# Splitting a third block product of the experts' first layer, with its sums on GpSimd

## The chip, the cores and the metric

The kernel runs on one core of a Trainium2 chip. Its time is device time in microseconds (us). The core has a matrix engine (TensorE, in the profile PE, its weight loads PEld), a vector engine (VectorE, DVE), a scalar engine (ScalarE, ACT), a general engine (GpSimd, POOL) and a queue engine (SyncE, SP). Matrix products go into PSUM banks, from which DVE and ACT read.

## The reference

The reference is one layer in float32 for 4096 tokens of width 512. A normalised `x` attends to 3202 rows of context, a gated sum is added to `x`, and a mixture of experts follows:

```python
xf = _layernorm(x).reshape(4096, 512)
gates = softmax(xf @ w_router + b_router)          # 8 experts
topv, topi = top_k(gates, 2)
cap = 640                                          # int(1.25 * 4096 / 8)
buf = each token's row into its expert's slots, up to cap
h = gelu(buf[e] @ w1[e] + b1[e])                   # 640 x 512 @ 512 x 2048
out = h @ w2[e] + b2[e]                            # 640 x 2048 @ 2048 x 512
y = the two outputs of each token, weighted by its gates and normalised
x = x + tanh(g_ffn) * y
```

The change touches the routing in one place, and otherwise the first of the two products of each expert, `buf[e] @ w1[e]`, and its gelu.

## The kernel before

The kernel has three stages in time. The attention takes the first 1480 us or so. The routing follows, to about 1577. Then come the experts, one after the other, each some 120 us, to about 2549.

**The routing.** The 32 tiles of 128 tokens are done in steps of 4, 4, 4, 4, 3, 3, 3, 3, 2 and 2 tiles (`STEPS`). For each tile `tile_mm` multiplies with the router and output weights (the PE rows `x1p`, L1755). For the step before, DVE picks the best two experts (`choose`, L1822 to L1843), and PE counts how many tokens each expert has so far with two small matmuls (`place`, L1870 and L1871, the second is `prev.counted`). POOL sends the rows to the experts' slots (L1904). The call `tc.issue_after` pins an instruction behind another on its engine; the order of PE's work in this stage is written with it. `idle_work(mm, n)` (L88) issues `n` matmuls 128x512 on constants behind `mm`; before the change it is used only where the first expert comes in.

**The experts' first layer.** It is computed transposed: `w1` is the weight operand, and the 640 slots, 320 at a time, are the moving operand. 2 x 2 blocks of `w1` and of the slots are multiplied with 7 block products in place of 8 (Strassen's scheme in Winograd's form), which needs sums of blocks of `w1` (`w1_sums`, L1652 to L1655) and of the slots (`x_forms`) beforehand, and sums of the products behind. A block product here is two program matmuls of 128x320, and the trace has two rows for each f32 matmul, so 4 rows. `hidden(e, idx)` does one step: all seven products for one 128-row block of each half of the output. There are eight steps, idx 0 to 7. In one step PE does the products in the order 0, 3, 4, 1, 5, 6, 2. They go to banks X, Q, Y, X, Z, Y and W. Three of the banks receive a copy before they are added to: ACT copies X into Y after product 0 (L2301), Y into Z after product 4 (L2310), and Z into W or into `hi` after product 5 (L2327). ACT also copies Q into `p5` (L2305), which DVE adds to the results (L2318, L2328, L2332), and does the gelus (L2315, L2325, L2329, L2335, L2336). Gelus that wait for a DVE sum are kept in a list `owed`; `due(n)` issues the first `n` of them.

**The products split deeper.** In steps 0 to 5 (`idx < DEEP_IDX`) the products 6 and 2 are not done step by step. A pair of steps (pair 0 to 3) is treated as a 2 x 2 problem again: seven program matmuls of 128x160 instead of eight of 128x320, in three stages `first`, `second` and `third` from `parts`, interleaved with the other products of steps 1 to 6 by `step(i)`. They need further sums: `deep_w` (L2210 to L2213, four of 128x128 for each pair and product) and `deep_x` (L2197 to L2200, four of 128x160 for each expert and product), all on DVE. Their results are copied by ACT (L2234, L2238) and added by DVE (L2246 to L2249). Steps 6 and 7 do the products 6 and 2 undivided for themselves, and no part of a split product is interleaved with step 7.

**The order.** Within the experts the order on PE, ACT and DVE and of the loads is written out by hand: `pe`, `ac`, `dv` and `ld` each append to a chain (`chained`), every instruction pinned behind the one before. POOL gathers the rows to be added to (`accs`, L2435) and scatters them at the expert's end (L2508).

**The first expert.** Its slots arrive while the routing ends. `first_expert_in` transposes them, does some early products, then DVE makes `x_forms` and the 20 small operations of `coefs(0)` (gate coefficients and row numbers, L2091 to L2094), and after those the deep sums of the first pair. The gathers of L2435 need the row numbers.

Of the kernel before, what the change touches and what calls it, by code (L numbers as in the profile page):

```python
# [9 lines left out]
ALU = mybir.AluOpType  # L10
# [4 lines left out]
P = 128  # L15
# [5 lines left out]
def gated_layer(ctx, tc, x, x_t, ctxt, ctxt_t, ctxt_c, ctxt_r, g_xattn, g_ffn, w_sim, w_sim_r, b_sim, W_qv, W_qv_t, b_qv, b_qv_c, w_router, b_router, w1, b1, w2, b2, out):  # L21
# [1638 lines left out]
    with ExitStack() as s2:  # L1660
# [279 lines left out]
        for g in range(len(STEPS)):  # L1940
            s.next = begin(g + 1) if g + 1 < len(STEPS) else None
            if prev is not None:
                choose(prev)
            ahead = min(3, s.n)
            for i in range(ahead):
                mm = tile_mm(s, i)
            if s.n > 2:
                with tc.issue_after(mm.ins):
                    place_prev()
                if s.n == G and routed:  # L1950
                    with tc.issue_after(scaled[-1].ins):
                        send(2)
                for i in range(ahead, s.n):
                    tile_mm(s, i)
            with tc.issue_after(scatters[-1]) if s.n == G and scatters else ExitStack():
                sc = scale(s)
            scaled.append(sc)
            if s.n == 2:
                with tc.issue_after(mm.ins):
                    place_prev()  # L1960
                mm = prev.counted
            if s.next is None:

                s.first = ps_mm.tile([P, 2, 512], F32, name="first", tag="mm")[:, 0, :E]
                with tc.issue_after(mm.ins):
                    mm = nc.tensor.matmul(s.first, ones, s.base[:, 0, :], start=True, stop=True)
            elif g + 2 == len(STEPS):

                cnt = ps_mm.tile([P, 2, 512], F32, name="cnt", tag="mm")[:, 0, :E]
                with tc.issue_after(mm.ins):  # L1970
                    mm = nc.tensor.matmul(cnt, ones, s.base[:, 0, :], start=True, stop=True)
                s.lift = small("lift", [P, s.n, E])
                stt(s.lift[:, 0, :], cnt, 1.0 / P, second, ALU.mult, ALU.max)
            with tc.issue_after(sc.ins):
                send(len(routed) if s.next is None else 4 if s.n == 2 else 7)
            prev, s = s, s.next
# [19 lines left out]
    with ExitStack() as s3:  # L1996
# [133 lines left out]
        def first_expert_in():  # L2130

            behind = None
            for s in range(NST):
                load = rows_in(0, s) if s else first_rows[0]
                row_loads.append(load.ins)

                near = (s + 1) * P <= CAP - len(late) // 2 * P
                if near:
                    tc.declare_no_dep(
                        load.ins, group="late" if s else "middle", reason="the last steps' rows lie behind these"  # L2140
                    )
                for i in scatters + (middle if s or not near else []) + ([] if near else late):
                    tc.add_manual_dep(
                        load.ins, i.name, mybir.DependencyInfo(mybir.DependencyClass.Sync, mybir.DependencyReason.DATA),
                        reason="every token is in its slot",
                    )
                if behind is None:

                    behind = prev.counted
                with tc.issue_after(behind.ins):  # L2150
                    ps = transposed(ps_tr, xb_of[0, s], f"bps0_{s}")
                dst = bT[:, :, s * P : (s + 1) * P]
                if s == NST // 2:
                    nc.scalar.copy(dst[:, :2, :], ps[:, :2, :])
                    with tc.issue_after(nc.vector.tensor_copy(dst[:, 2:, :], ps[:, 2:, :]).ins):
                        w_ops.pop(0)()
                else:
                    (nc.vector.tensor_copy if s % 2 else nc.scalar.copy)(dst, ps)
                behind = moved[-1] if s else idle_work(moved[-1], 2)
                for cols, q, f in WORK.get(s, ()):  # L2160
                    B = [bT[:, k, :HC] for k in ((2, 3) if q else (0, 1))]
                    behind = early_product(q, f, B, cols, behind, cols.start > 0)
            tail["pe"] = behind
            for op in x_forms():
                tail["dv"] = op()
            dv(*coefs(0))

        first_expert_in()
        with tc.issue_after(row_loads[-1]):
# [4 lines left out]
        def rows_of(ti, s):  # L2174
# [9 lines left out]
            k: (b, [flat_set[i][:, q * HH : (q + 1) * HH] for q in range(3)] + [p7[:, i - 5, :HH]])  # L2184
            for k, i, b in (("2", 5, xT[2]), ("6", 6, B22))
        }

        def w_of(k, pair):
            n = 3 * (2 * (pair % 2) + (k == "6"))
            return [flat_set[2 + (n + q) // 4][:, (n + q) % 4 * P : ((n + q) % 4 + 1) * P] for q in range(3)]  # L2190

        def deep_x(k):

            b, (t1, t2, t4, t3) = x_of[k]
            b11, b12, b21, b22 = (b[:, c, d : d + HH] for c in range(2) for d in (0, HH))
            return [
                lambda: tt(t1, b12, b11, ALU.subtract),  # L2197
                lambda: tt(t2, b22, t1, ALU.subtract),
                lambda: tt(t3, b22, b12, ALU.subtract),
                lambda: tt(t4, b21, t2, ALU.subtract),  # L2200
            ]

        def deep_w(e, k, pair):

            a = w1_forms(e, pair // 2)[int(k)]
            f = pair % 2 * 2 * P
            a11, a12, a21, a22 = (a[:, c, f + r : f + r + P] for r in (0, P) for c in range(2))
            s1, s2, s4 = w_of(k, pair)
            return [
                lambda: tt(s1, a21, a22, ALU.add),  # L2210
                lambda: tt(s2, s1, a11, ALU.subtract),
                lambda: tt(a21, a11, a21, ALU.subtract),
                lambda: tt(s4, a12, s2, ALU.subtract),  # L2213
            ]

        def parts(e, k, pair, c_bank):

            XWQ = ps_tr.tile([P, DC, P], F32, name=f"d{e}_{k}{pair}", tag="tr").rearrange("p c t -> p (c t)")
            X, W, Q = (XWQ[:, i * HH : (i + 1) * HH] for i in range(3))
            YZ = banks[c_bank][:, : 2 * HH]  # L2220
            Y, Z = YZ[:, :HH], YZ[:, HH:]
            a = w1_forms(e, pair // 2)[int(k)]
# [2 lines left out]
            s1, s2, s4 = w_of(k, pair)  # L2225
            b, (t1, t2, t4, t3) = x_of[k]
            b11, _, b21, b22 = (b[:, c, d : d + HH] for c in range(2) for d in (0, HH))
            dst = hT[:, 0, 2 * pair : 2 * pair + 2, HC:] if k == "6" else hT[:, 1, 2 * pair : 2 * pair + 2, :HC]

            def first():  # L2230
                mm(X, a11, b11, True, True)
# [9 lines left out]
            def third():  # L2241
                mm(Z, s3, t3, False, True)
                mm(Y, s4, b22, False, True)

            adds = [
                lambda: tt(dst[:, :, HH:], dst[:, :, HH:], Q.unsqueeze(1).to_broadcast([P, 2, HH]), ALU.add),  # L2246
                lambda: tt(dst[:, :, :HH], dst[:, :, :HH], XWQ[:, : 2 * HH].rearrange("p (f t) -> p f t", f=2), ALU.add),
                lambda: tt(dst[:, 0, HH:], dst[:, 0, HH:], Y, ALU.add),
# [2 lines left out]
                    Z.unsqueeze(1).to_broadcast([P, 2, HH]), ALU.add,  # L2251
                ),
            ]
            return first, second, third, adds, dst

        def hidden(e, idx):

# [11 lines left out]
            if 1 <= idx <= DEEP_IDX:  # L2269
                k, pair = ("6", idx // 2) if idx % 2 else ("2", idx // 2 - 1)  # L2270
                part = parts(e, k, pair, 5 if split else 2 + (idx + 1) % 2)

            def product(ps, k, start=False):
                for i in range(2):
                    mm(ps, A[k][i], XS[{2: 6, 6: 2}.get(k, k)][i], start and i == 0, i == 1)

            def step(i):
                if part:
                    part[i]()

# [15 lines left out]
            else:  # L2296
# [4 lines left out]
                    ac(lambda: nc.scalar.copy(Y, X))  # L2301
                step(0)
                due(1)
                product(Q, 3, True)
                ac(lambda: nc.scalar.copy(p5, Q))  # L2305
                step(1)
                if not part:
                    due(1)
                product(Y, 4)
                ac(lambda: nc.scalar.copy(Z, Y))  # L2310
                step(2)
                due(1)
            if not there:
                product(X, 1)
                ac(lambda: nc.scalar.activation(lo[:, :HC], X, AF.Gelu, bias=b_lo))  # L2315
            due(len(owed))
            if split:
                dv(lambda: tt(lo[:, HC:], Y, p5, ALU.add))  # L2318
# [108 lines left out]
        for e in range(E):  # L2427
# [2 lines left out]
                ld(lambda: load_w2(e, 0), lambda: load_w2(e, 1))  # L2430
            b2_t = sb.tile([P, D], F32, name=f"b2_{e}", tag="b2", bufs=1)
            ld(lambda: nc.sync.dma_start(b2_t, b2[e].partition_broadcast(P)))
            cf, ti = cf_of[e], ti_of[e]
            for s in range(NST):
                gather = nc.gpsimd.indirect_dma_start(  # L2435
# [12 lines left out]

            (B11w, B12w, B21w, B22w), right, inner = output(e)
            bias = [add(s, slice(None), b2_t) for s in range(NST)]  # L2450
            dv(*deep_w(e, "6", 0), *deep_x("6"))
            if e:
                dv(*w1_sums(e, 0, 2))
            for idx in range(2 * KQ):
                if more and idx == 2:
                    ld(*[lambda s=s: rows_in(e + 1, s) for s in range(NST - 1)])
# [6 lines left out]
                    dv(*deep_w(e, "2", 0), *deep_x("2"))  # L2463
                if idx in (1, 3):
                    dv(*deep_w(e, "6", 1 + idx // 2), *deep_w(e, "2", 1 + idx // 2))
                if idx in (4, 6, 7):
                    k = (0, 2, 4)[(4, 6, 7).index(idx)]
                    dv(left(1, k, k + 2), left(3, k, k + 2))
# [175 lines left out]
```

## Time and profile before

| | |
|---|---|
| median of three runs | 2552.36 us (2552.12 to 2552.47) |
| profiled execution | 2551.32 us, span 2549.5 us |
| busy time of TensorE, VectorE, ScalarE, GpSimd | 2531.7, 1974.8, 715.8, 275.5 us |
| mean granted TensorE clock | 0.999 |

The profile is of one execution. In the views by instruction a row gives the start from the span's beginning, the time from start to end, the engine, the line in the kernel, the operation, the tile written and the tile read, the shape, and how many neighbouring instructions of the same kind are merged into it (x8). A bracket behind it tells how long the engine was idle before and which engine's instruction ended that. Matmul rows overlap one another, so the distance between starts is what one costs, not the row's own duration. In the table by stretches the columns are the busy time of PE, PEld, DVE, ACT and POOL with the number of instructions, the granted clock of TensorE as a share of full speed, the share of the DMA engines, and the GB/s moved.

### The profile page before, as it was taken

The page shows a single profiled execution, that of the slowest core. Times are in us where ns is not written, and L with a number is a line of the kernel's source. Part 1 is how long each engine was busy: PE and PEld are TensorE (multiplying, and loading weights), DVE is VectorE, ACT ScalarE, POOL GpSimd, SP SyncE. Part 2 cuts the span into 40 slices and gives each one's busy share as a digit, 9 for nine tenths or more (in the row PEclk, how much of TensorE's full clock was granted, in tenths as well). Part 3 has the DMA queues.
Part 4 walks back from the last instruction along what each step waited for, and adds up shares of the span by engine and source line. Part 5 has one row for each costly group of instructions (what it writes and reads, how often), then busy time and mean ns, then how long its engine had stood idle before and what let it go on. Part 6 is the DMA issues. An engine that isn't in the chain of part 4 may idle for free.

```text
span 2549.5 us, 37831 instructions
## 1 busy us (share of the span) xinstructions
PE 2531.7 (99%) x14256; PEld 2214.7 (87%) x14256; DVE 1974.8 (77%) x4118; ACT 715.8 (28%) x1556; POOL 275.5 (11%) x399
## 2 busy tenths in 40 slices
PE   9999999999999999999999999999999999999998
PEld 7788888998988988989989887798888888888978
DVE  8887865876967868859658657887888888787877
ACT  1112302323123123123231144424232332424150
POOL 0101220001001000000000056010101010101010
PEclk9999999999999999999999999999999999999999
DMA  7568795875976957758748895322313141414120
GB/s 265 194 215 295 268 350 175 281 266 167 317 226 205 307 194 241 265 188 285 249 154 292 272 353 190 130 100 95 133 67 133 71 156 43 162 42 158 47 103 21
DMA packets 198407, 489.08 MB, mean 192 GB/s; under 512 B 22462, under 2 KB 79102, under 8 KB 196176
## 3 DMA queue, kind: packets, MB, share of 16 engines
q1 hardware_dynamic: 151984, 386.37, 45.0%
q0 software_dynamic: 21696, 59.07, 6.4%
q10 hardware_dynamic: 24544, 41.21, 4.4%
q8 instruction: 113, 1.85, 0.3%
q14 instruction: 70, 0.57, 0.1%
HBM read 397.40 MB, written 97.52 MB: 194 GB/s over the span
## 4 chain that ended last, share of the span: by engine, by line
PE 89%; issue 5%; DVE 4%; POOL 1%; DMA 1%; ACT 0%; POOLq 0%; SPq 0%; DVEq 0%
PE bank L2027 30%; PE bank L761 21%; PE bank L984 13%; PE bank L1153 6%; PE bank L1510 5%; PE x1p L1755 2%; PE bank L1254 2%; PE d L2027 2%; PE p7d L1510 1%; PE p4d L1510 1%; PE bank L813 1%; PE v L1254 1%; PE bps L2103 1%; DVE SM L1023 1%; PE bank L990 1%
## 5 line engine op out<-in xcount | busy, mean ns | idle before, releaser
L761 PE MATMUL bank<-Qp,kt 128*128 128x256 f32 x1344 | 305.2, 379 | 0.0
L761 PEld LDWEIGHTS bank<-Qp,kt 128*128 128x128 f32 x1344 | 254.4, 190 | 34.1
L2027 PE MATMUL bank<-w,hT 128*128 128x256 f32 (+1 forms) x1280 | 260.7, 359 | 0.7 <-ACT u L2519 0.7
L2027 PEld LDWEIGHTS bank<-w,hT 128*128 128x128 f32 x1280 | 223.8, 190 | 27.4 <-ACT u L2519 1.1
L761 PE MATMUL bank<-q,kt 128*128 128x256 f32 x1008 | 231.3, 379 | 0.0
L761 PEld LDWEIGHTS bank<-q,kt 128*128 128x128 f32 x1008 | 191.5, 190 | 26.0
L2027 PE MATMUL bank<-bT,w 128*128 128x320 f32 x736 | 211.1, 432 | 0.6 <-ACT bank L2310 0.6
L984 PE MATMUL bank<-dt,vf 128*128 128x128 f32 x1680 | 204.8, 275 | 0.0
L984 PEld LDWEIGHTS bank<-dt,vf 128*128 128x128 f32 x1680 | 196.0, 192 | 0.0
L2027 PEld LDWEIGHTS bank<-bT,w 128*128 128x128 f32 x736 | 136.6, 190 | 50.5 <-ACT bank L2310 1.1
L2027 PE MATMUL bank<-XT,w1s 128*128 128x320 f32 x512 | 156.4, 433 | 0.1
L804 DVE TENSOR_TENSOR M<-M,E_all 128x1024 f32<-128x1024 f32 x80 | 97.9, 1223 | 46.0 <-ACT E_all L721 44.6
L2508 POOL DMA_INDIRECT out<-acc,ti x40 | 39.7, 992 | 806.7 <-DVE acc L2447 800.0
L1755 PE MATMUL x1p<-W,q2T 128*128 128x264 f32 x512 | 117.7, 391 | 3.0 <-DVE lg L1777 1.8
L717 DVE TENSOR_TENSOR E_all<-bank,p5s 128x512 f32<-128x512 f32 x42 | 28.9, 688 | 113.4 <-ACT bank L716 113.3
L1755 PEld LDWEIGHTS x1p<-W,q2T 128*128 128x128 f32 x512 | 97.7, 192 | 20.1 <-PE pos L1871 1.8
L2027 PEld LDWEIGHTS bank<-XT,w1s 128*128 128x128 f32 x512 | 91.9, 190 | 25.9 <-ACT bank L2286 0.5
L891 DVE TENSOR_TENSOR E_all<-E_all,mb 128x1024 f32<-128x1024 f32 x84 | 101.2, 1211 | 10.3 <-ACT mb L866 10.3
L984 PE MATMUL bank<-E_all,vf 128*128 128x128 f32 x828 | 106.5, 275 | 0.0
L892 ACT ACTIVATE E_all<-E_all 128x1024 f32<-128x1024 f32 x84 | 88.8, 1057 | 49.8 <-DVE E_all L891 49.3
L984 PEld LDWEIGHTS bank<-E_all,vf 128*128 128x128 f32 x828 | 99.8, 192 | 0.3
L2027 PEld LDWEIGHTS bank<-l,l 128*128 128x128 f32 x736 | 92.9, 192 | 7.6
(644 smaller groups left out, 4955.1 us busy)
## 6 DMA issues: line engine op xcount, KB each, us to landing
vf<-vf_d SPq DMA_DIRECT2D x122, 768.0 KB
kt<-kt_d SPq DMA_DIRECT2D x84, 512.0 KB
w<-in_w SPq DMA_DIRECT2D x16, 2048.0 KB
w<-in_w SPq DMA_DIRECT2D x32, 1024.0 KB
kt<-in_ctxt_t SPq DMA_DIRECT2D x84, 384.0 KB
wp<-wt_d SPq DMA_DIRECT2D x56, 520.0 KB
buf_d<-zero SPq DMA_DIRECT2D x80, 129.0 KB
xb<-buf_d SPq DMA_DIRECT2D x39, 258.0 KB
```

The source lines that it names most:

```text
L717: tt(dst(1, 1), Z, p5, ALU.add)
L761: nc.tensor.matmul(ps[:, jl, :], kts[j][:, KSLOT[p], k, :], B[p][:, k, :], start=start and jl == 0 and k == 0, stop=stop and k == 1, skip_ ...
L804: tt(M, M, e[:, :, h], ALU.max)
L891: live[g]["last"] = tt(e, e, m, ALU.subtract)
L892: live[g]["exp"] = nc.scalar.activation(e, e, AF.Exp)
L984: nc.tensor.matmul(ps, a[:, j, :], rhs[r][:, j, :], start=start and j == 0, stop=j == NP - 1 and (rest is None or add is None), skip_group ...
L1153: nc.tensor.matmul(ps[b], vt[:, j - i * JH, b * P : (b + 1) * P], right(j) if j < NJ else right_c, start=start and j == 0 and b == 0, stop ...
L1254: mm = nc.tensor.matmul(acc[k][:, b, :], a[:, b * P : (b + 1) * P], r, start=start and b == 0, stop=stop, skip_group_check=True,)
L1510: nc.tensor.matmul(ps[m], A[p][:, k, m * P : (m + 1) * P], wt[:, k, :], start=start and k == 0, stop=stop and k == DC - 1, skip_group_chec ...
L1755: mm = nc.tensor.matmul(ps[:, j, :B1], qTs[g][:, c, q * P : (q + 1) * P], W1[:, c, j, :], start=(c == 0), stop=(c == DC - 1))
L2027: return chained("pe", lambda: nc.tensor.matmul(ps, a, b, start=start, stop=stop, skip_group_check=True))
L2508: sc = nc.gpsimd.indirect_dma_start(out=out[:, :], out_offset=rows_of(ti, s), in_=accs[s][:, :], in_offset=None, bounds_check=N - 1, oob_i ...
```

## The change

It has three parts.

The first is in the experts' first layer. Product 3 is split deeper in the same way as products 6 and 2, for pairs 1, 2 and 3 of every expert but the first, and for pairs 2 and 3 of the first: 23 pairs. Its three stages (`extra`) are all done in the even step of the pair, interleaved with the rest, and product 3 into Q is left out in both steps. Its results go into both `p5` buffers by three more ACT copies and two more DVE adds (in place of the two copies of Q). Its sums are made by GpSimd in a chain of its own (`gp`): four of 128x160 at each expert's start and four of 128x128 for each pair, ahead of and behind the gathers and between them. In the steps concerned only one owed gelu is issued ahead of `lo`'s gelu, and all others behind it.

The second is the first expert's order on DVE: the deep sums of its first pair now come before `coefs(0)`, not behind.

The third is in the routing: where a step of 3 tiles follows one of 4, one `idle_work` matmul is issued behind the count `prev.counted`.

```diff
@@ routing
                 with tc.issue_after(mm.ins):
                     place_prev()
+                if prev is not None and prev.n > s.n:
+                    mm = idle_work(prev.counted, 1)
@@ first_expert_in
             for op in x_forms():
                 tail["dv"] = op()
-            dv(*coefs(0))
@@ deep sums
+        flat_low = [t.rearrange("p a b -> p (a b)") for t in sets[0]]
+        x_of["3"] = (xT[0], [flat_low[6][:, q * HH : (q + 1) * HH] for q in range(3)] + [u2[:, 0, :HH]])
+
+        def third_split(e, idx):
+            return idx >= (KQ if e == 0 else 2)
...
-        def deep_x(k):
+        def deep_x(k, tt=tt):
...
-        def deep_w(e, k, pair):
+        def deep_w(e, k, pair, tt=tt):
@@ parts
-            X, W, Q = (XWQ[:, i * HH : (i + 1) * HH] for i in range(3))
+            X, W, Q = (XWQ[:, i * HH : (i + 1) * HH] for i in ((2, 0, 1) if k == "3" else (0, 1, 2)))
...
+            def copies():
+                nc.scalar.copy(p5s[1], XWQ[:, : 2 * HH])
+                nc.scalar.copy(p5s[0][:, :HH], X)
+                return nc.scalar.copy(p5s[0][:, HH:], Q)
+
             adds = [
+                lambda: tt(p5s[0][:, HH:], p5s[0][:, HH:], Y, ALU.add),
+                lambda: tt(
+                    p5s[1].rearrange("p (d t) -> p d t", d=2), p5s[1].rearrange("p (d t) -> p d t", d=2),
+                    Z.unsqueeze(1).to_broadcast([P, 2, HH]), ALU.add,
+                ),
+            ] if k == "3" else [
@@ hidden
+            triple = third_split(e, idx)
+            extra = parts(e, "3", idx // 2, 1) if triple and idx % 2 == 0 else None
...
             def step(i):
+                if extra:
+                    extra[i]()
                 if part:
                     part[i]()
...
                 step(0)
                 due(1)
-                product(Q, 3, True)
-                ac(lambda: nc.scalar.copy(p5, Q))
-                step(1)
-                if not part:
-                    due(1)
+                if not triple:
+                    product(Q, 3, True)
+                    ac(lambda: nc.scalar.copy(p5, Q))
+                    step(1)
+                    if not part:
+                        due(1)
                 product(Y, 4)
                 ac(lambda: nc.scalar.copy(Z, Y))
-                step(2)
-                due(1)
+                step(1 if triple else 2)
+                if not triple:
+                    due(1)
             if not there:
                 product(X, 1)
                 ac(lambda: nc.scalar.activation(lo[:, :HC], X, AF.Gelu, bias=b_lo))
+            if triple:
+                step(2)
+            if extra:
+                ac(extra[5])
+                dv(*extra[3])
             due(len(owed))
@@ the loop over experts
+            if e:
+                dv(*deep_w(e, "6", 0), *deep_x("6"), *w1_sums(e, 0, 2))
+
+            def third_w(pair):
+                return chained("gp", *deep_w(e, "3", pair, nc.gpsimd.tensor_tensor))
+
+            chained("gp", *deep_x("3", nc.gpsimd.tensor_tensor))
+            if third_split(e, 2):
+                third_w(1)
+            if e == 0:
+                dv(*deep_w(0, "6", 0), *deep_x("6"), *coefs(0))
             cf, ti = cf_of[e], ti_of[e]
             for s in range(NST):
                 gather = nc.gpsimd.indirect_dma_start(
...
-            dv(*deep_w(e, "6", 0), *deep_x("6"))
-            if e:
-                dv(*w1_sums(e, 0, 2))
...
                     dv(*deep_w(e, "6", 1 + idx // 2), *deep_w(e, "2", 1 + idx // 2))
+                if idx in (3, 5):
+                    third_w(1 + idx // 2)
```

More of the change, by code (lines that the diff above doesn't have):

```diff
@@ L2186, in gated_layer @@
         }
+        flat_low = [t.rearrange("p a b -> p (a b)") for t in sets[0]]
+        x_of["3"] = (xT[0], [flat_low[6][:, q * HH : (q + 1) * HH] for q in range(3)] + [u2[:, 0, :HH]])
+        def third_split(e, idx):
+            return idx >= (KQ if e == 0 else 2)
         def w_of(k, pair):
+            if k == "3":
+                return [flat_low[4 + pair % 2][:, q * P : (q + 1) * P] for q in range(3)]
             n = 3 * (2 * (pair % 2) + (k == "6"))
             return [flat_set[2 + (n + q) // 4][:, (n + q) % 4 * P : ((n + q) % 4 + 1) * P] for q in range(3)]
-        def deep_x(k):
+        def deep_x(k, tt=tt):
             b, (t1, t2, t4, t3) = x_of[k]
@@ L2227, in parts @@
             b11, _, b21, b22 = (b[:, c, d : d + HH] for c in range(2) for d in (0, HH))
-            dst = hT[:, 0, 2 * pair : 2 * pair + 2, HC:] if k == "6" else hT[:, 1, 2 * pair : 2 * pair + 2, :HC]
+            dst = None if k == "3" else hT[:, 0, 2 * pair : 2 * pair + 2, HC:] if k == "6" else hT[:, 1, 2 * pair : 2 * pair + 2, :HC]
             def first():
@@ L2253, in parts @@
             ]
-            return first, second, third, adds, dst
+            return first, second, third, adds, dst, copies
         def hidden(e, idx):
```

## The prediction

> **What bounds the kernel now.** I read the page first, for the engines' shares and the clock, then the table by stretches of the span, then the instructions in order of time at the three places that the change touches. The page and the table, the table's columns being the busy time of PE, PEld, DVE, ACT and POOL, the granted clock, and DMA:
>
> ```profile
> PE 2531.7 (99%) x14256; PEld 2214.7 (87%) x14256; DVE 1974.8 (77%) x4118; ACT 715.8 (28%) x1556; POOL 275.5 (11%) x399
> ...
> 2000.00:2500.00 500.00, 499.32 (x2843) 426.04 (x2842) 412.84 (x911) 161.20 (x410) 40.68 (x40) 1.00 0.26 95
> ```
>
> TensorE is the bound, and in the experts it has no gaps: 499.32 us of 500, with VectorE busy for 412.84 and GpSimd for 40.68. So matmul time taken out there is worth its full length, as long as no new wait opens. In the same way every new wait of PE costs its full length; nothing lies behind PE to absorb it. So I look for each bank that a matmul must wait for after the change. Step 7 of the second expert's first layer (`hidden(e, 7)`, the last unsplit step), in order of time:
>
> ```profile
> 1757.04 2.32 PE L2027 MATMUL bank<-XT,w1s 128*128 128x320 f32 x8
> 1757.24 0.41 ACT L2301 COPY bank<-bank 128x320 f32<-128x320 f32 x1 [2.82 <-PE bank L2027]
> ...
> 1759.19 2.32 PE L2027 MATMUL bank<-bT,w 128*128 128x320 f32 x8
> 1759.39 0.41 ACT L2310 COPY bank<-bank 128x320 f32<-128x320 f32 x1
> ...
> 1760.47 0.53 ACT L2315 ACTIVATE hT<-bank,b_t 128x320 f32<-128x320 f32 x1 [0.19 <-PE bank L2027]
> 1760.90 0.55 ACT L2335 ACTIVATE hT<-hT,b_t 128x320 f32<-128x320 f32 x1
> ...
> 1761.35 0.52 ACT L2336 ACTIVATE hT<-bank,b_t 128x320 f32<-128x320 f32 x1
> 1761.90 0.41 ACT L2327 COPY bank<-bank 128x320 f32<-128x320 f32 x1
> ...
> 1762.42 1.01 PE L2027 MATMUL bank<-XT,w 128*128 128x320 f32 x3
> ```
>
> The reader should see two things. The eight rows from 1757.04 are product 3 (into Q) and product 4 (onto Y). Product 4 needs Y, which ACT copies out of X until 1757.65; product 3 hides that. And the last copy, of Z into W, ends at 1762.31, only 0.12 before its matmuls start at 1762.42: ACT is just in time here, although two of its five owed gelus (L2325) ran earlier in the step.
>
> **Durations of PE.** One f32 matmul of the program is two rows. Eight rows of width 320 take 2.15 us (1757.04 to 1759.19), .2692 a row; the start distance at width 160 is .1358. After a wait the first rows take .104 longer (.373 against .269).
>
> **Part 1, the third product.** A pair of steps has product 3 twice: 8 x .2692 = 2.153 us. Split deeper it is 7 program matmuls of width 160: 14 x .1358 = 1.901. That is .252 us less per pair; 2 pairs in the first expert and 3 in each of the other seven make 23, so -5.80 us. With each goes work for the others. ACT has five copies in place of two: per pair about 1.5 us against .85, in idle time (161.20 of 500). DVE has two more adds, .32 + .49, hidden in its 87 idle us of 500 but moving other adds back by .8 per pair. GpSimd has 16 sums per expert (12 in the first) that are not in the trace in this form.
>
> The wait that it adds, first place: step 7 has no part of a deep product to put between, since parts are issued in steps 0 to 6. Without product 3 it goes from product 0 straight to product 4, which waits for the copy of Y. PE would be free where product 3 starts now, 1757.040; the copy ends at 1757.650, and PE restarts .053 after such a copy elsewhere (1592.907 to 1592.960), so at 1757.703. That is .663 + .104 = .767 us, in each of 8 experts. In steps 3 and 5 the other part's first stage (six rows of 160, .81) covers the .663 with .15 over; steps 2, 4 and 6 have two stages there.
>
> Second place, same step: only one owed gelu is issued after product 0; the other four now stand behind `lo`'s gelu. Let T0 be the start of product 5 (1760.27 now). `lo`'s gelu starts at T0 + .20, the four at T0 + .63, 1.07, 1.52 and 1.97 (distances .426, then .445 to .452), the last ends at T0 + 2.49, and the copy of Z into W runs from T0 + 2.52 to 2.93. Product 2 starts at T0 + 2.98 instead of T0 + 2.153 (8 rows): .83 + .104 = .93 us, again 8 times. Queued behind that copy on ACT is the gelu of `hi`, needed only in the second layer's later products; nothing else waits. Bounds for the two together: at least the two bare gaps, 8 x 1.49 = 11.9; at most, with ACT 5% slower, 8 x 1.85 = 14.8. I take 8 x 1.70 = +13.6.
>
> **GpSimd's sums.** The nearest rows are a MEMSET of 128x260, 317 ns, and of 128x512, 559 ns, which read nothing, and a TENSOR_TENSOR of 128x4 with a `pow`, about 1050 ns. Below, at memset speed, a 128x160 sum is about .2 us; above, 1.05. The sums read two operands, as L2197 on DVE does in .32, so I take .45, between these. The first that PE needs (`s2` of pair 1) is needed at 1721.2 in the second expert; behind the gathers at 1.3 us each it is there by 1718.6 to 1719.5. At 1.05 each, the six up to it add 6 x .6 = 3.6 and it comes 1.0 to 1.9 us late. I cost it at nothing: the cover is the 1.7 to 2.6 us left, and if that goes PE waits in step 2, seven times, up to +13 us; below nothing there is no reason for. The scatters and gathers on the same queue move back by four to six sums, 1.8 to 2.7 us; the gathers start at 1715.4 in the second expert and their rows are first used at 1756.8 (L2447), so that is hidden.
> The trace shows no wide GpSimd sum beside a DVE sum. The Trainium skill, "SBUF — State Buffer", section "Who interferes with whom", says that a DVE instruction with two SBUF inputs contends with a GpSimd instruction reading SBUF, one blocking for the whole of the other. This speaks against the change: an estimate from it is that GpSimd's 16 sums could each hold DVE for their length, some 7 us of its 20 idle us per expert, so the sum would still stand unless a late add meets PE.
>
> **Part 2, the first expert.** The chain of waits there, and PE's rows:
>
> ```profile
> 1594.04 0.22 DVE L2094 SCALAR_TENSOR_TENSOR cf<-dc,cf,SX 128x1 f32<-128x1 f32 x1
> ...
> 1594.66 0.43 ACT L2286 COPY bank<-l 128x320 f32<-128x320 f32 x1
> ...
> 1595.52 0.54 PE L2027 MATMUL d<-l,l 128*128 128x160 f32 x2 [0.95 <-issue]
> ...
> 1596.35 0.54 PE L2027 MATMUL d<-l,w1s 128*128 128x160 f32 x2 [0.29 <-DVE p L2199]
> ...
> 1596.73 1.24 PE L2027 MATMUL bank<-XT,w1s 128*128 128x320 f32 x4
> ```
>
> The 20 small coefficient operations hold DVE from 1591.89 to 1594.25; the deep sums, on which the two PE waits rest (1.11 and .46 by starts), end at 1596.30. Moved ahead they are done 2.32 earlier, at 1593.98, before PE can ask (1594.41). Late next is ACT: its copy of the early product ends at 1595.10, so product 3 or 4 starts at about 1595.15 rather than 1596.73 (-1.58). Of this a later copy, queued behind a gelu whose add DVE doesn't do sooner, gives back about .35, and GpSimd's four sums, now beside the deep sums, some .3. I take -.9, between 0 (the sums held by GpSimd as long as by the coefficients) and -1.6. The first expert's five gathers on POOL wait for the coefficients, 2.3 us longer; their rows are used in step 5, some 40 us on.
>
> **Part 3, the matmul on constants in routing.** Two stretches, one window of the clock long each:
>
> ```profile
> 1506.25:1509.66 3.41, 1.48 (x7) 0.81 (x6) 3.03 (x17) 2.23 (x6) 2.56 (x3) 1.00 1.04 427
> 1509.66:1513.08 3.42, 3.21 (x7) 2.53 (x8) 3.04 (x15) 2.20 (x6) 2.49 (x4) 0.50 1.01 390
> ```
>
> After a stretch with PE busy for 1.48 the clock was granted at 0.50 for 3.41 us; the next lowest stretches on the same grid, 2.24, 2.31 and 2.44, were followed by 1.00. In the slow stretch the router's rows stand .44 apart instead of .222: 6 x .218 + .351 = 1.66 us lost. The new matmul (128x512, 2 x .429) runs after the count (L1871) at 1508.88 and is over before 1509.87, where PE next has work, so it costs nothing, and lifts 1.48 to 2.34, among the unthrottled. I take -1.66; bounds 0 (still throttled) and -1.7, and +.1 if it should end late.
> The Trainium skill, "TensorE: Matmul & The Clock Gate", in its part on the two states, calls the 3413 ns window free-running; this trace agrees with the length (3.41). By it the grid falls elsewhere in each run, so a run that is not throttled would have nothing to gain; by the rule alone the term may be anything between 0 and the full loss.
>
> **Sum.** -5.80 + 13.58 - .9 - 1.66 = +5.2 us. The profiled execution took 2551.32 (span 2549.5), the median of the runs is 2552.36, 1.04 more. So about 2556.5 for a profiled execution and 2557.6 for the median. A measurement of this kernel tells about 0.2% (5.1 us, 2547.3 to 2557.5) from no change, and the forecast lies on that edge.
>
> **Rivals.**
> 1. One of step 7's waits is covered: gelus that overlap more closely, say. The row for it is the copy into W that is just in time now; against it stands that four ACT instructions of .445 can't fit in 2.15 with `lo`'s gelu and a copy. The sum falls by 6.1 to 7.4: 2550.2 to 2551.5. Within.
> 2. Both are covered, or the scheduler keeps something between: -5.80 - .9 - 1.66 = 2544.0, faster. It decides only if step 7's product 4 doesn't wait for the copy of Y; against it, ACT stood idle for 2.82 us and began the copy .20 after product 0, so nothing on ACT could bring it earlier.
> 3. GpSimd's sums are late, because they take over .75 to .88 us (.45 and a sixth of the cover), or are held that long by DVE: 1 to 1.9 us of waiting in step 2 of seven experts, 2564.6 to 2570.9, slower.
> 4. Step 7 as forecast, but the clock still drops and the first expert gains little: 2559.5 to 2560.2.
>
> **Chances.** The forecast .48 (its own range 2555.5 to 2559.3, half above the edge), rival 1 .16, rival 2 .10, rival 3 .14, rival 4 .12. The range leaves out most of rival 2 and the upper end of rival 3: 2549 to 2567. Slower: .24 + .14 + .12 = .50; within: .24 + .14 = .38; faster: .12 with the lower end of rival 1.
>
> **What would show it.** In step 7 of each expert, PE rows of product 4 with .6 to .8 us idle behind ACT's copy of Y, and of product 2 with .8 to .9 behind the copy of Z; 14 rows of 160 in place of 8 of 320 in 23 places; no throttled stretch near 1510; the first expert's PE without waits for DVE. Wrong it is if PE waits for POOL (rival 3), or if step 7 has no such gaps.

## The result and the profile after

The changed kernel takes 2560.75 us (median of 7 runs, 2560.16 to 2563.55), the kernel before 2552.33 on the same chip. The ratio is 1.0038, 95% interval 1.0028 to 1.0048 (the ratios given here are worked out from all the runs and need not be the quotient of the medians, here 1.0033). By the medians it is slower by 8.4 us, where 5.2 were forecast. The time lies inside the stated range.

TensorE is still the bound, but the experts have gaps now. From the page, and from the table by stretches (columns: the stretch, its length, then the busy time of PE, PEld, DVE, ACT and POOL, the granted clock, DMA):

```profile
PE 2533.9 (99%) x14396; PEld 2224.5 (87%) x14396; DVE 2005.2 (78%) x4164; ACT 724.9 (28%) x1625; POOL 357.2 (14%) x523
...
2000.00:2500.00 500.00, 494.13 (x2883) 425.00 (x2882) 423.00 (x937) 168.59 (x454) 81.30 (x104) 1.00 0.27 95
```

Of 500 us PE is busy for 494.13, where it was 499.32. The table of waits names the two gaps, each eight times, once per expert (total, times, longest):

```profile
PE bank L2029 <- ACT bank L2358: 5.4, 8, 0.7
PE bank L2029 <- ACT bank L2325: 4.0, 8, 0.5
```

These are idle times counted from the modelled ends of the matmuls. By start distances a gap costs more, as the instructions in order of time show for step 7 of the second expert:

```profile
1762.31 0.41 ACT L2325 COPY bank<-bank 128x320 f32<-128x320 f32 x1 [2.82 <-PE bank L2029]
...
1762.77 1.34 PE L2029 MATMUL bank<-XT,w1s 128*128 128x320 f32 x4 [0.50 <-ACT bank L2325]
...
1765.23 0.53 ACT L2341 ACTIVATE hT<-bank,b_t 128x320 f32<-128x320 f32 x1 [0.67 <-PE bank L2029]
1765.65 1.00 ACT L2356 ACTIVATE hT<-hT,b_t 128x320 f32<-128x320 f32 x2
...
1766.56 0.55 ACT L2366 ACTIVATE hT<-hT,b_t 128x320 f32<-128x320 f32 x1
1767.01 0.51 ACT L2367 ACTIVATE hT<-bank,b_t 128x320 f32<-128x320 f32 x1
1767.56 0.41 ACT L2358 COPY bank<-bank 128x320 f32<-128x320 f32 x1
...
1768.02 0.81 PE L2029 MATMUL bank<-XT,w 128*128 128x320 f32 x2 [0.67 <-ACT bank L2358]
```

Product 4 starts .05 after ACT's copy of Y. Four owed gelus (L2356 twice, L2366, L2367) stand between `lo`'s gelu and the copy of Z into W, and product 2 starts behind that copy. Against the regular start distance the first gap is .662 to .663 in every expert and the second .835 to .841, each with .104 more in the row after it.

Where the profiled execution's 12.2 us came from, by PE's starts in both traces:

| stretch | before | after | difference |
|---|---|---|---|
| start to the first 128x320 matmul (attention, routing, first slots) | 1589.95 | 1593.18 | +3.23 |
| from there to the first expert's second layer | 53.54 | 54.78 | +1.24 |
| seven times from second layer to second layer | 840.34 | 848.03 | +7.69 |
| from the last expert's second layer to the end | 65.71 | 65.78 | +.07 |

The first line isn't typical. The profiled execution was the longest of the seven runs (2563.55), and the clock dropped in it for longer than in the profile before (6.83 us against 3.41). If the other three lines hold in the median too, 8.4 - 1.24 - 7.69 - .07 leaves about -.6 for that stretch; that is an estimate.

Two more places of the changed kernel. In the first expert DVE's sums take longer beside GpSimd's:

```profile
1594.20 0.98 POOL L2206 TENSOR_TENSOR l<-XT,l 128x160 f32<-128x160 f32 x1
...
1594.72 1.14 DVE L2077 TENSOR_TENSOR XT<-bT,XT 128x640 f32<-128x640 f32 x1
1595.14 1.10 POOL L2207 TENSOR_TENSOR u<-XT 128x160 f32<-128x160 f32 x1
...
1595.79 0.60 DVE L2218 TENSOR_TENSOR l<-w1s 128x128 f32<-128x128 f32 x1
1596.20 0.57 POOL L2208 TENSOR_TENSOR l<-XT,l 128x160 f32<-128x160 f32 x1
1596.43 0.49 DVE L2219 TENSOR_TENSOR l<-l,w1s 128x128 f32<-128x128 f32 x1
1596.85 0.28 DVE L2220 TENSOR_TENSOR w1s<-w1s 128x128 f32<-128x128 f32 x1
...
1602.63 0.54 PE L2029 MATMUL bank<-p,w1s 128*128 128x160 f32 x2 [0.94 <-ACT bank L2314]
```

The sum of 128x640 (L2077) takes 1.14 us, where the kernel before takes .82; the deep sum of 128x128 takes .60 beside GpSimd and .28 alone. PE's wait for DVE is shorter than it was, and a new one of 1.1 us by starts, behind ACT, follows (L2314). The ACT copies there stand behind a gelu (L2360) that had waited 2.15 us for a DVE add, so DVE's delay is passed on. In the routing, by stretches again, the drop of the clock near 1510 is gone, and there is one from 1555.59 on:

```profile
1552.18:1555.59 3.41, 1.29 (x8) 0.82 (x6) 3.00 (x16) 1.95 (x6) 2.80 (x3) 1.00 0.79 302
1555.59:1559.00 3.41, 2.70 (x6) 2.16 (x7) 2.99 (x19) 1.83 (x5) 2.50 (x4) 0.50 0.49 177
```

### The profile page after: what moved, and what is told of

The parts are those of the page before. It is cut to its first block, busy times and chain, and to the rows that moved or that the text cites. A ratio compares the mean times of both kernels' runs of the same rounds, so it can differ in the third digit from the quotient of the medians.

```text
span 2561.8 us, 38527 instructions
## 1 busy us (share of the span) xinstructions
PE 2533.9 (99%) x14396; PEld 2224.5 (87%) x14396; DVE 2005.2 (78%) x4164; ACT 724.9 (28%) x1625; POOL 357.2 (14%) x523
## 4 chain that ended last, share of the span: by engine, by line
PE 88%; DVE 4%; issue 4%; DMA 1%; ACT 1%; POOL 1%; POOLq 0%; SPq 0%; DVEq 0%
PE bank L2029 29%; PE bank L761 21%; PE bank L984 13%; PE bank L1153 6%; PE bank L1510 5%; PE d L2029 3%; PE bank L1254 2%; PE x1p L1755 1%; PE p7d L1510 1%; PE p4d L1510 1%; PE bank L813 1%; PE v L1254 1%; DMA buf_d<-xn,sidx 1%; POOL buf_d L1904 1%; PE bps L2105 1%
## 5 line engine op out<-in xcount | busy, mean ns | idle before, releaser
L2029 PE MATMUL bank<-bT,w 128*128 128x320 f32 x736 | 217.3, 432 | 0.6 <-ACT bank L2335 0.6
L2029 PE MATMUL bank<-l,l 128*128 128x128 f32 (+1 forms) x782 | 108.9, 279 | 0.0
L2029 PEld LDWEIGHTS bank<-l,l 128*128 128x128 f32 x782 | 100.4, 192 | 7.6
L2029 PE MATMUL bank<-XT,w1s 128*128 128x320 f32 x328 | 101.5, 436 | 4.1 <-ACT bank L2325 4.0
```

The lines of the kernel that those rows point to most:

```text
L2029: return chained("pe", lambda: nc.tensor.matmul(ps, a, b, start=start, stop=stop, skip_group_check=True))
```

## The experiments

Every kernel was timed in turn with the kernel before. The ratios are to the kernel before, with 95% intervals. Theory A was that the two waits of step 7 cost the time; its rivals were that GpSimd's sums, or the two other parts, did.

### The third product alone

```diff
-                if prev is not None and prev.n > s.n:
-                    mm = idle_work(prev.counted, 1)
...
-                dv(*deep_w(0, "6", 0), *deep_x("6"), *coefs(0))
+                dv(*coefs(0), *deep_w(0, "6", 0), *deep_x("6"))
```

> The kernel before with the split third product alone: the first expert's coefficients stay ahead of its deep sums, and the idle matmul in routing is not issued. Theory A (the two waits of step 7 cost the time): the trace of the changed kernel has 8 x (.767 + .941) = 13.7 us of these waits, the split saves 5.8, and what its sums on GpSimd cost elsewhere is small (.24 in each of seven experts, 1.7): 7.9 to 9.6 us over the kernel before. Theory B (the surplus over the forecast comes from the other two parts, which did harm): 5 to 6 us over, with the rest of the 8.4 in the other parts.

Measured: 2561.98 against 2552.36 us, ratio 1.0037 (1.0023 to 1.0050), so +9.6. This is the upper end of theory A: the loss is that of the third product, and the other two parts do no harm that can be measured. The first expert takes 55.77 us to its second layer. The kernel before has 53.54; the split takes .50 off and the two gaps add 1.71; 1.03 is left. That is what GpSimd's sums cost here: beside them DVE's four sums of 128x640 take .65 longer and its coefficients .42, and PE waits for a DVE sum for 2.18 us by starts, where it was 1.11:

```profile
1597.10 0.54 PE L2027 MATMUL d<-l,l 128*128 128x160 f32 x2 [2.02 <-DVE l L2203]
```

### The two other parts without the third product

```diff
+                if prev is not None and prev.n > s.n:
+                    mm = idle_work(prev.counted, 1)
...
-            dv(*coefs(0))
...
+            dv(*deep_w(e, "6", 0), *deep_x("6"))
+            dv(*(w1_sums(e, 0, 2) if e else coefs(0)))
...
-            dv(*deep_w(e, "6", 0), *deep_x("6"))
-            if e:
-                dv(*w1_sums(e, 0, 2))
```

> The two other parts without the third product: first expert's deep sums ahead of its coefficients, and the idle matmul in routing. Theory A1 (in the changed kernel GpSimd's four sums held the first expert's DVE sums, so that the reordering gained nothing there): without them the reordering is worth its -1.2 us, the first expert has no PE wait for DVE, and with the routing's part 1.2 to 2.9 us under the kernel before. Theory B (the reordering itself gains nothing, whoever runs beside it): within .3 us of what the routing part alone makes, and a PE wait of about 1 us in the first expert behind ACT or DVE.

Measured: 2551.09 us, ratio .9995 (.9986 to 1.0004): not told from the kernel before. The trace tells more. The first expert takes 52.80 us to its second layer, .74 less than before, and PE goes through the deep product with no wait for DVE:

```profile
1595.31 0.43 PE L2029 MATMUL d<-bT,w1s 128*128 128x160 f32 x2
1595.58 0.43 PE L2029 MATMUL d<-l,l 128*128 128x160 f32 x2
1595.85 0.43 PE L2029 MATMUL d<-l,w1s 128*128 128x160 f32 x2
```

So the reordering gains .74 where no GpSimd sum runs beside it, where 1.2 was expected. Counted from the first full-width matmul, the full-width product behind the deep one starts 1.58 us earlier, as the prediction had it. But it starts after a wait, which costs .10 in the row behind it, and two later waits behind ACT's copies (.26 and .27, each with .10 in the row behind it) give back .74 more. In the routing the clock dropped at 1556, not at 1510.

### The gelus of step 7 spread as before

```diff
-                due(1)
+                due(1 if part or not triple else 2)
...
-                if not triple:
+                if not triple or not part:
                     due(1)
```

> The changed kernel with the owed gelus of step 7 spread as before: two behind the copy of Y, one behind the copy of Z, two behind lo's gelu. Theory A: the wait ahead of product 2 (.837 + .104 a step) goes, the one ahead of product 4 stays: 8 x .94 = 7.5 us under the changed kernel, so about 1 us over the kernel before. Theory B (GpSimd's sums or the DVE they hold set step 7's end): the waits move but PE's time stays within 1 us of the changed kernel.

Measured: 2553.40 us, ratio 1.0004 (.9995 to 1.0013): 7.35 under the changed kernel. In the trace the gap ahead of product 2 is gone in all eight experts, and the one ahead of product 4 is .662 to .663, as it was. Theory A gave 7.5.

### Product 0 of step 7 ahead of product 2 of step 6

This has the spread gelus too.

```diff
-                else:
+                elif idx < 2 * KQ - 1:
                     product(X, 0, True)
                     ac(lambda: nc.scalar.copy(Y, X))
...
+                if idx == 2 * KQ - 2:
+                    last = [a[:, k, (KQ - 1) * P : KQ * P] for a in w1_forms(e, 1)[:1] for k in range(2)]
+                    y_last = banks[2 + (idx + 1) % 2][:, :HC]
+                    for i in range(2):
+                        mm(X, last[i], XS[0][i], i == 0, i == 1)
+                    ac(lambda: nc.scalar.copy(y_last, X))
                 product(W, 2)
```

> As the spread gelus, and product 0 of step 7 issued ahead of product 2 of step 6, so that ACT's copy of Y runs beside product 2. Theory A: both waits go, 8 x 1.71 = 13.7 us under the changed kernel, and so 4 to 5.5 us under the kernel before: the split's 5.8 less what the sums on GpSimd cost. Theory B (the time is bound elsewhere, or DVE and GpSimd take over as the next limit): less than half of that.

Measured: 2546.97 us, ratio .9979 (.9970 to .9988), 13.8 under the changed kernel (the kernel before took 2552.33 beside the one and 2552.36 beside the other) and 5.4 under the kernel before. On another chip, against 2552.42 us for the kernel before:

> The version with spread gelus and product 0 of step 7 ahead of product 2 of step 6, run again on the chip of the version with pinned sums: 53.1 us in the first expert's first layer, .8 us longer than with the pinned sums if theory A1 holds; 5 us or so under the kernel before.

There it took 2546.75, ratio .9978 (.9969 to .9988). Both gaps of step 7 are gone. Its first profile, steps 6 and 7 and then the stretch by table:

```profile
1754.87 1.24 PE L2029 MATMUL bank<-bT,w 128*128 128x320 f32 x4
1755.94 1.24 PE L2029 MATMUL bank<-XT,w 128*128 128x320 f32 x4
...
1756.14 0.41 ACT L2369 COPY bank<-bank 128x320 f32<-128x320 f32 x1 [1.74 <-PE bank L2029]
```

```profile
2000.00:2500.00 500.00, 499.27 (x2952) 434.28 (x2952) 432.25 (x943) 164.49 (x446) 81.18 (x104) 1.00 0.26 95
```

The copy of Y (L2369) runs while PE does product 2 of the step before, and PE is busy for 499.27 of 500 again, with DVE at 432.25. From second layer to second layer it takes 119.33 to 119.6 us, where the kernel before took 120.05 and the changed one 121.0 to 121.3. The 23 pairs' saving is there, .72 at best for the three pairs of an expert against .76 worked out.

### GpSimd's sums in the first expert only

```diff
-                return chained("gp", *deep_w(e, "3", pair, nc.gpsimd.tensor_tensor))
+                return None if e else chained("gp", *deep_w(e, "3", pair, nc.gpsimd.tensor_tensor))
...
-            chained("gp", *deep_x("3", nc.gpsimd.tensor_tensor))
+            if not e:
+                chained("gp", *deep_x("3", nc.gpsimd.tensor_tensor))
```

> The changed kernel, with GpSimd's sums for the split third product made only in the first expert (12 of the 124 sums); experts 2 to 8 multiply the first one's sums again, so their results are not those of the layer, while every matmul, copy and add stays. Theory A (the sums cost only what their traces show beside the two waits of step 7): from the start of one expert's second layer to the next, 120.9 to 121.05 us against 121.0 to 121.3 now, so 1 to 1.7 us under the changed kernel in all. Theory B (DVE held by GpSimd in the later experts is a main part of the 8.4 us): 4 us or more under the changed kernel.

Measured: 2562.85 us on a chip where the kernel before takes 2555.13; ratio 1.0027 (1.0016 to 1.0038) against 1.0038 (1.0028 to 1.0048) with all the sums, so the two intervals overlap. The sums of the later experts are left out here, and the output is not the layer's. By the trace, 121.00 to 121.06 us from second layer to second layer, 847.14 for the seven against 848.03: the sums of the later experts cost .9 us in all, just under the 1 to 1.7 of theory A. The rival asked for 4 or more. Where the .9 is can be read in DVE's groups of `w1_sums`, first before, then after (the mean in ns is the figure behind the busy time):

```profile
L1654 DVE TENSOR_TENSOR w<-w 128x256 f32<-128x256 f32 x60 | 25.1, 418 | 0.0
```

```profile
L1654 DVE TENSOR_TENSOR w<-w 128x256 f32<-128x256 f32 x60 | 31.4, 524 | 0.0
...
L2221 POOL TENSOR_TENSOR l<-w1s,l 128x128 f32<-128x128 f32 x23 | 22.0, 958 | 0.0
```

GpSimd's sums of the next expert's weights run beside these; without them L1654 takes 428 ns. In four of the changed kernel's experts PE then has a wait of .13 to .15 us, and .10 more in the row after it, in the second layer behind an ACT copy (at 1706, 1828, 1949 and 2312 us). Without the sums the wait there is .02, with the same .10, in all seven. Compared row by row, this place makes .11 to .13 more in those four experts and .10 to .17 less in the other three, and two others in the second layer make about .06 more each in nearly every expert. So the .9 is a balance of several places; how each comes from the sums isn't shown.

### The routing's part alone

The kernel before with the two lines on `idle_work`.

> The kernel before with the idle matmul of the routing alone. Theory C1 (the clock drop moves): three profiles with the idle matmul have no slow rows near 1510 but 7 to 12 slow rows from 1555 on, behind a longer wait of PE; so within .8 us of the kernel before, and slow rows near 1556. Theory C2 (as forecast): 1.0 to 1.7 us under the kernel before, and no slow rows in the routing.

Measured: 2553.25 against 2555.13 us, ratio .9998 (.9989 to 1.0007): C1, though with 5 slow rows and not 7 to 12. Its profile has none near 1510. Near 1555 PE waits for 2.21 us, where the kernel before waited for .54, and rows at half clock, .440 apart, follow:

```profile
1550.77 1.28 PE L1755 MATMUL x1p<-W,q2T 128*128 128x264 f32 x5
1554.26 0.37 PE L1870 MATMUL pos<-mask,upper 128*128 128x24 f32 x2 [2.21 <-issue]
...
1555.98 4.37 PE L1755 MATMUL x1p<-W,q2T 128*128 128x264 f32 x12 [0.79 <-issue]
```

PE was not held up at 1510, so it is done with its tiles at 1552.05, where the kernel before was at 1553.00, and waits for the same count of the next step (in the changed kernel's table of waits this is L1870 behind DVE's L1829, 2.0 us). The drop comes with that wait: over all twelve profiles this wait is 1.16 to 2.31 us in seven, and six of them have the drop behind it; in the five where it is .54 to .59 there is none there. What one part gives, the next takes.

### GpSimd's sums of the first expert behind its gathers

First they were only put later in the code:

```diff
-            chained("gp", *deep_x("3", nc.gpsimd.tensor_tensor))
+            if e:
+                chained("gp", *deep_x("3", nc.gpsimd.tensor_tensor))
...
             stored.clear()
+            if e == 0:
+                chained("gp", *deep_x("3", nc.gpsimd.tensor_tensor))
```

> The version with spread gelus and product 0 of step 7 ahead of product 2 of step 6, and in the first expert GpSimd's four sums of the slots behind its gathers. Theory A1 (those four sums hold DVE's deep sums in the first expert): no PE wait for DVE at its start, and from its first full-width matmul to its second layer 52.3 us against 53.1 with the sums ahead; .8 us under the version without this, 6 us under the kernel before. Rival (the limit there is ACT's copies): unchanged, 53.1.

Measured: 2548.93 against 2555.13 us, ratio .9977 (.9968 to .9986), and 53.11 us in the first expert, as without the edit. That says nothing on the theory: in the trace the sums still run ahead of the gathers, from 1589.4 on. With the first of the sums pinned behind the last gather (`tail["gp"] = gather`):

> The version with spread gelus and product 0 ahead, with GpSimd's four sums of the slots pinned behind the last gather of the first expert (in the version before this, where they only stood later in the code, the order on GpSimd stayed as it was, sums first). Theory A1 (these sums hold DVE's sums): DVE's four sums of the slots take .82 each (two took 1.15 beside GpSimd's) and the first deep sum .28 (.60), PE waits for neither DVE nor ACT's copy of the deep product for more than .5 us, and from the first full-width matmul to the second layer the first expert takes 52.3 us against 53.1, .8 us less. Rival (ACT's copies are the limit there): 53.1.

Measured: 2547.59 us, ratio .9980 (.9971 to .9989). In the timing it can't be told from the version with the sums ahead on the same chip (2546.75). In the trace the first expert takes 52.67 us against 53.11, and DVE has its old durations:

```profile
1591.43 0.82 DVE L2077 TENSOR_TENSOR XT<-bT,XT 128x640 f32<-128x640 f32 x1
...
1592.16 0.28 DVE L2218 TENSOR_TENSOR l<-w1s 128x128 f32<-128x128 f32 x1
...
1601.65 0.71 DVE L1652 TENSOR_TENSOR w1s<-w 128x256 f32<-128x256 f32 x1
...
1608.15 0.28 ACT L2242 COPY bank<-d 128x160 f32<-128x160 f32 x1 [1.16 <-DVE hT L2268]
```

PE's waits for DVE's deep sums and the 1.1 us behind ACT's copy are gone, down to three of .25 to .29 us behind ACT. So GpSimd's sums did hold DVE there. The gain is .44, not the .8 expected. The two other parts alone, less the split's .50, would give 52.30; the .38 that remains is the third of these waits, at 1608.48 (.256, and .104 in the row after it), which that version doesn't have. The ACT copy ahead of it (L2242) waited for a DVE add. The sums moved behind the gathers now run beside DVE's L1652 to L1655, which take .63 to .74 us each, where they take .41 to .43 with no GpSimd sum beside them. So the rows point to GpSimd here too, at another place, and not to a limit of ACT; no run tests that by itself.

### One more idle matmul, ahead of the drop near 1556

```diff
                     mm = nc.tensor.matmul(cnt, ones, s.base[:, 0, :], start=True, stop=True)
+                mm = idle_work(mm, 1)
                 s.lift = small("lift", [P, s.n, E])
```

> The same with one more idle matmul in routing, behind the count ahead of the last step of 2 tiles, where PE is idle for 1.04 us just before the slow rows near 1556. If the clock drops there because PE was busy for too little of the stretch before (1.82 and 1.49 us of 3.41), the stretch comes to about 2.7, no row is slow, and the kernel is .5 to 1.7 us faster than without it. If the later part of routing waits for DVE in any case, the slow rows go and the time stays within .4 us.

Measured: 2549.32 us, ratio .9980 (.9971 to .9989), against .9977 without it: no difference. There are no slow rows near 1556 in its profile, but there are some near 1513 again. The clock's own record changes at 1512.64; in the stretch up to there PE, with the idle matmul in it, was busy for 2.19:

```profile
1509.23:1512.64 3.41, 2.19 (x8) 1.25 (x9) 3.10 (x14) 2.35 (x6) 2.53 (x3) 1.00 1.02 423
1512.64:1516.05 3.41, 3.41 (x10) 2.59 (x9) 2.88 (x18) 1.83 (x5) 2.43 (x4) 0.50 1.01 353
```

Over the ten profiles with the idle matmul behind the step of 4 tiles, slow rows begin near 1511 or 1513 in two, between 1555 and 1559 in six, and in two there are none. One kernel shows both: the version with product 0 ahead has slow rows from 1555 in its first profile and none in its second. The two profiles without the idle matmul have them near 1510. If the stretches of 3.41 us are laid so that they end where the clock's record changes, as here, PE was busy for .92 to 2.19 us in the ten ahead of these drops. But a stretch of 1.62 (1592.96 in the run of the third product alone) and one of 1.76 (1549.40 in the second profile with product 0 ahead) were followed by the full clock. So the drop depends on more than the busy time of one stretch, and its rule stays open. The two profiles with no slow rows take 151.31 and 151.57 us from the first row `x1p` to the first 128x320 matmul, where the two without the idle matmul take 152.29 and 151.99. So even with no drop at all the routing gains .4 to 1.0 us by these traces, not 1.66.

## Why the prediction was right or wrong

The verdict, slower by more than 0.2%, was given .50, and it came so. The mechanism of the forecast held where it counted most, in step 7; what lay beside it was less well sized. The stated range is 18 us wide, so that the time lies in it says little. The forecast's own narrower range, 2555.5 to 2559.3 with .48, was missed; 2560.75 lies just above rival 4, which had .12.

**The two waits of step 7** were forecast at 8 x 1.70 = 13.6 us. Measured are .663 + .104 and .837 + .104 by starts, 8 x 1.708 = 13.7, and the runs that take them away one after the other gain 7.35 and 13.8. Rivals 1 and 2, one wait or both covered, fell. In the later experts no other step of the first layer has a gap above .08 us, as the prediction had said of steps 2 to 6. Product 4 did wait for the copy of Y, and the four gelus took the time that their spacing in the profile before gave.

**The saving of the split** was put at 5.80. With the waits gone it shows: .72 of .76 per expert in the best experts, .45 in those with 119.6 us.

**GpSimd's sums** were costed at nothing, with .45 us each. They take .50 to .96 on average by line, 1.1 beside a DVE sum of 128x640. PE was never seen waiting for them, so rival 3 fell in the form in which it was put. But they hold DVE: .9 us over the seven later experts, and about .8 in the first. The Trainium skill in "SBUF — State Buffer", section "Who interferes with whom", says that DVE instructions with two SBUF inputs contend with GpSimd's reads, and these rows bear it out (1.14 against .82, .60 against .28). That one is held for the whole of the other they don't show: L2077 overlaps two GpSimd sums of .98 and 1.10 and takes .32 longer. The prediction weighed it for all the experts alike and took .3 for the first; it mattered most there, where DVE is on the path.

**The first expert** was forecast at -.9: -1.58 for the earlier start, .35 given back by a later copy, and .3 for GpSimd's sums. Two of these terms were too small. Without the sums the reordering gives -.74, not -1.23: .84 is given back, not .35. And beside GpSimd's sums nothing is left of it: 54.78 - 53.54 is +1.24, and the split and the gaps make +1.20 of that. So the sums cost about .8 by difference, 1.03 in the order of the third product alone, not .3; .44 of it was won back by moving four of them.

**The idle matmul** was forecast at -1.66, on the ground that the stretch would then be among the unthrottled. In the changed kernel's profile it is (2.24 us busy between 1507.80 and 1511.21, clock 1.00 behind it), but in two other profiles it isn't (2.16 and 2.19, both followed by half clock). The step that failed is that nothing would come behind it: PE came sooner to a wait for DVE 45 us later, and the clock mostly dropped there; alone the part gives .9998 (.9989 to 1.0007). "TensorE: Matmul & The Clock Gate" in the Trainium skill, in its part on the two states, says that the window runs free of the kernel; the same kernel with and without slow rows agrees with that. The prediction itself said that the term may be anything between 0 and the full loss, and still entered it in full.

The median missed the forecast by 3.15 us: .9 in the first expert, about 1.1 in the routing (1.66 less the .6 that the median leaves) and 1.1 in the seven later experts (7.69 measured against 6.6), .9 of it from GpSimd's sums. Rival 4, the clock still dropping and the first expert gaining little, with 2559.5 to 2560.2, is the case that came, with GpSimd's .9 on top.

## What to carry to other kernels

Where a matmul accumulates onto a bank that another engine copies first, the product between the two hides that copy: before a product is taken out, look in every step for what else covers the copy, above all in the last step, which has nothing left to interleave. Here moving one product of the last step ahead by one product, and spreading the activations as before, turned 8.4 us slower into 5.4 us faster than the kernel before. And where two engines take turns on the path, as PE and DVE do in this routing, filling a gap on the one can move the wait to the next place where it meets the other.

## What the runs showed of the hardware

GpSimd's sums of two operands and DVE's slow one another when they run at the same time: a GpSimd sum of 128x160 took .52 us beside DVE operations of 128x1 (at 1593.48 in the run of the third product alone) and up to 1.11 beside DVE's 128x640, which in turn took 1.14 to 1.15 instead of .82. A GpSimd sum of 128x128 with no DVE instruction beside it took .44 to .47. After a drop the granted clock stayed at half for 3.41 or 6.83 us, 5 to 12 rows of 128x264, and these stood .440 us apart instead of .222. The row after the first one behind a wait of PE came .104 us late, at 128x320 and at 128x160 alike.
